# Layer 1 of a two-layer graph attention network: the norm's statistics, W2's last columns and the softmax placed differently

## The chip, the cores and the metric

The kernel runs on one core of one Trainium2 chip. The metric is the device time of one execution in microseconds; the median of 15 runs is given. The core has TensorE (PE; its weight loads are listed as PEld), VectorE (DVE), ScalarE (ACT), GpSimd (POOL) and SyncE (SP), which each work through their own instructions in order and wait for one another by semaphores, and 16 DMA engines.

## The reference

There are 10,000 nodes with 768 features and 170,000 edges (80,000 in both directions and a self loop per node; the network adds a second self loop). One layer of the reference is, cut to what matters:

```python
xl = (x @ W).reshape(n, heads, out_ch)
e = leaky_relu(alpha_src[src] + alpha_dst[dst], 0.2)
e = exp(e - segment_max(e, dst)[dst]);  alpha = e / segment_sum(e, dst)[dst]
out = segment_sum(xl[src] * alpha, dst)

h = gat_conv(x, ..., heads=4, out_ch=256)           # layer 1: 1024 columns
h = relu(layer_norm(h)) + x @ Wr1
h1 = h
h = gat_conv(h, ..., heads=1, out_ch=768)           # layer 2
h = layer_norm(h) + h1 @ Wr2
x = layernorm(x + h)
```

## The kernel before

All arithmetic is in float32. First, x @ W1 is computed for all nodes and stored row by row in a table in DRAM (`table1`: 1024 columns, 4 + 4 attention terms, one number of order), while the nodes are sorted by their number of edges. From then on a *tile* is 128 nodes of like degree, one per partition. There are 79 tiles. A tile has as many *rows* (`SLOTS[t]`) as its largest degree needs; row k of a tile is one gathered table row per node, 128 x 1033 numbers. Tiles are taken in an order in which the sizes first rise (8, 10, 11, ... 26, 41) and then fall (27, ... 11, 9).

Layer 1 (`ordered_layer1`) goes through the tiles in one long unrolled program, whose order on each engine is the order in which it is written (`tc.manual_schedule()`); the tile pools add only the waits. For tile t:

- Rows come through a ring of 29 slots (`Ring`, `RING1`). `ring.fetch` issues a gather on GpSimd's queue (L424) for a row 29 ahead as soon as a row is used up.
- `weights_of(t)` makes the softmax over all rows of a tile: `logits` (L477 to L489: sum, leaky, maximum, difference, exponential on ScalarE, then the rows' numbers are turned into slots for layer 2 and the ring's last columns are set to a large negative number) and `normalised` (L496 to L502). It is started three rows before the end of the tile in front (`LEAD = 3`).
- The first `on_pe(t)` rows are weighted and summed by TensorE: ScalarE makes diagonal matrices (L727), TensorE multiplies them with the rows into `acc` in PSUM (L733).
- The other rows are added to `acc` by VectorE (`weigh`). One row in four VectorE weighs itself, in four instructions (L519); the other three, *shared*, ScalarE scales first (`multiply`, L508) and VectorE adds in one instruction (L515). ScalarE scales at most three rows ahead.
- When tile t's rows are summed, its norm is made at the head of tile t + 1: `deviation` (L577, L579 on VectorE; L581, L582 on ScalarE), `scaled` (L591, L593) and the ReLU with the residual (L804). TensorE transposes the result (`halves`, L705; ScalarE copies it out, L706), multiplies by W2 (L826) and ScalarE copies the two parts (512 and 258 columns) into `row` (`store`, L763), which SP's queue writes to `table2` for layer 2. TensorE also transposes the next tile's x and multiplies it by Wr1 (`product`, L171).

PSUM is full: `acc` has two buffers of two banks, the residual one of two banks, and `half`, which holds transposes and W2's products, two of one bank.

The lines by which the head of a tile is ordered are:

```python
stats = deviation(small, pieces(means[:, :C1], BANK))
...
store(t - 2)
...
xT, moves = from_x(t)
multiplied(first + 2)
...
scaled(h, [means[:, :C1]], stats, g1_b, be1_b)
nc.vector.scalar_tensor_tensor(h, h, 0.0, r_before[:, :C1], op0=OP.max, op1=OP.add)
for move in moves: move()
multiplied(first + LEAD)
```

Layer 2 works in the same manner on `table2` and isn't touched.

Of the kernel before, what the change touches and what calls it, by code (L numbers as in the profile page):

```python
# [35 lines left out]
P = 128  # L36
# [10 lines left out]
RING1 = 29  # L47
RING2 = 41
LEAD = 3
DIAGONALS = 5  # L50
ON_PE2 = 512
SHARE = 4
# [27 lines left out]
def gnn_kernel(ctx, tc, x, x_cols, src, dst, src_col, dst_col, W1, a_src1, a_dst1, b1, g1, be1, Wr1, br1,  # L80
# [390 lines left out]
    def logits(small, ring, lo, hi, ad, heads, c, top=None):  # L471


        n = hi - lo
        e = small.tile([P, ring.size, heads], F32, name="e")[:, :n]
        for a, b, rows in ring.parts(lo, hi):
            nc.vector.tensor_tensor(e[:, a - lo:b - lo], rows[:, :, c + heads:c + 2 * heads],  # L477
                                    ad[:, None, :].to_broadcast([P, b - a, heads]), op=OP.add)
        leaky(e, e)
        new = small.tile([P, heads], F32, name="new")  # L480
        nc.vector.reduce_max(new, e.rearrange("p k h -> p h k"), axis=AX.X)
        if top is not None:
            nc.vector.tensor_max(new, new, top)
        nc.vector.tensor_tensor(e, e, new[:, None, :].to_broadcast([P, n, heads]), op=OP.subtract)  # L484
        nc.scalar.activation(e, e, AF.Exp)  # L485
        for a, b, rows in ring.parts(lo, hi):
            if not ring.own:
                nc.vector.tensor_scalar(slots[:, a:b], rows[:, :, R1 - 1], -1.0, float(NP), op0=OP.mult, op1=OP.min)
                nc.vector.memset(rows[:, :, c + heads:], -BIG)  # L489
        return e, new  # L490

    def normalised(small, e, heads, t):
# [76 lines left out]
    def pieces(a, width):  # L569

        return [a[:, c:c + width] for c in range(0, a.shape[1], width)]

    def deviation(small, parts):

        st = small.tile([P, len(parts), 6], F32, name="st")
        for j, a in enumerate(parts):
            nc.vector.bn_stats(st[:, j, :], a)  # L577
        mv = small.tile([P, 2], F32, name="mv")
        nc.vector.bn_aggr(mv, st.rearrange("p k s -> p (k s)"))  # L579
        sd = small.tile([P, 1], F32, name="sd")  # L580
        nc.scalar.activation(sd, mv[:, 1:2], AF.Ln, bias=eps)  # L581
        nc.scalar.activation(sd, sd, AF.Exp, scale=-0.5)  # L582
        return mv[:, 0:1], sd

    def scaled(to, parts, mean_and_deviation, g, b):

        mean, inv = mean_and_deviation
        c = 0
        for a in parts:
            d = c + a.shape[1]  # L590
            nc.vector.scalar_tensor_tensor(to[:, c:d], a, mean, g[:, c:d], op0=OP.subtract, op1=OP.mult)  # L591
            c = d
        nc.vector.scalar_tensor_tensor(to, to, inv, b, op0=OP.mult, op1=OP.add)  # L593

# [88 lines left out]
    def ordered_layer1():  # L683
        nc.scalar.add_instruction(mybir.InstLoadActFuncSet(name=nc.get_next_instruction_name(), act_func_set_id=6, engine=nc.scalar.engine))
        with tc.tile_pool(name="b1", bufs=1) as pool, tc.tile_pool(name="small1", bufs=2) as small, \
# [32 lines left out]
            def on_pe(t):  # L718


                return min(max(SLOTS[t] // 2 - 5, 1), ON_PE1, SLOTS[t])

            def summed(acc, diagonals, e, q, lo, hi, m):

# [23 lines left out]
                    yield acc  # L748

            def shared(t, k):  # L750
                return (k - on_pe(t)) % SHARE > 0

            last = None
            full = None
            ready = []
            ahead = iter(())

            def store(t):

                nonlocal full  # L760
                row = pool.tile([P, R2], F32, name="row")
                for c, q in full:
                    nc.scalar.copy(row[:, c:c + q.shape[1]], q)  # L763
                full = None
                nc.sync.dma_start(table2[TURNS[t] * P:(TURNS[t] + 1) * P, :], row)


            xT, moves = from_x(0)
            for move in moves:
                move()  # L770
# [1 line left out]
            for t in range(NT + 1):  # L772
# [4 lines left out]
                if whole and not ready:  # L777
                    ahead = weights_of(t)
                    ready += itertools.islice(ahead, 2)

                def multiplied(upto):
                    nonlocal done
                    while whole and done < min(upto, n):
                        if shared(t, done):
                            multiply(ring.slot(FIRST[t] + done), e[:, done], DH1)
                        done += 1

                if whole:
                    e, acc = ready
                if last:  # L790
                    r_before, means = last
                    stats = deviation(small, pieces(means[:, :C1], BANK))
                for _ in ahead:
                    pass
                if full is not None:
                    store(t - 2)
                moves = []
                if live and t:
                    xT, moves = from_x(t)
                multiplied(first + 2)  # L800
                if last:
                    h = pool.tile([P, C1], F32, name="h")
                    scaled(h, [means[:, :C1]], stats, g1_b, be1_b)
                    nc.vector.scalar_tensor_tensor(h, h, 0.0, r_before[:, :C1], op0=OP.max, op1=OP.add)  # L804
                for move in moves:
                    move()
                multiplied(first + LEAD)
                if last:
                    hT = pool.tile([P, K1, P], F32, name="hT")
                    events = [(first + j, move) for j, move in enumerate(halves(hT, h))]  # L810
                def by_wr1():
                    nonlocal r
                    if live and t:
                        r = product(xT, wr1, C1, ps_r)
# [2 lines left out]
                    by_wr1()  # L817

                def to_layer2():
                    nonlocal full  # L820
                    nc.sync.dma_start(h1_d[t - 1], hT.rearrange("p k n -> p (k n)"))
                    full = []
                    for c in range(0, R2, BANK):
                        q = ps_half.tile([P, BANK], F32, name="half")[:, :min(BANK, R2 - c)]
                        for j in range(K1):
                            nc.tensor.matmul(q, hT[:, j, :], w2[:, j, c:c + q.shape[1]],  # L826
                                             start=(j == 0), stop=(j == K1 - 1))
                        full.append((c, q))

                if last:  # L830
                    events.append((first + 2, to_layer2))
# [8 lines left out]
                def due(k):  # L840
                    while events and events[0][0] <= k:
                        events.pop(0)[1]()

                if live and not whole:
                    due(first + 1)
                    sums, acc = (ps_acc.tile([P, 2 * BANK], F32, name="acc") for _ in range(2))
# [11 lines left out]
                                 [by_wr1, lambda: due(n)] + [lambda: None] * n)  # L858
                ready = []
                ahead = iter(())  # L860
                if whole and t + 1 < NT and SLOTS[t + 1] + LEAD <= ring.size:
                    ahead = weights_of(t + 1)
                for k in range(n if whole else 0):
                    multiplied(k + 1 + LEAD)
                    if n - LEAD <= k < n - LEAD + 2:
                        ready += itertools.islice(ahead, 1)
                    if k >= first:
                        weigh(acc, ring.slot(FIRST[t] + k), e[:, k], DH1, shared=shared(t, k))
                    ring.fetch(FIRST[t] + k + 1 + ring.size)
                    due(k)  # L870
                due(DEGREES)
                ready += itertools.islice(ahead, max(2 - len(ready), 0))
                last = None
                if live:
                    last = r, acc
            store(NT - 1)

    def ordered_layer2():
        nonlocal ps_big
# [406 lines left out]
```

## Time and profile before

| | |
|---|---|
| median of 15 runs | 5630.83 us (5619.23 to 5651.92) |
| profiled execution | 5617.48 us, of which the program's span is 5615.6 us |
| mean granted TensorE clock | 0.928 |
| layer 1 within the span | about 906 to 3407 us |
| L515, VectorE adds a scaled row | 801 times, 985.7 us, mean 1231 ns |
| L508, ScalarE scales a quarter of a row | 3284 times, 1341.6 us, mean 523 ns |
| L727 and L733, diagonals and their products | 956 of 389 ns; 1912 passes of 409 ns |
| L577 and L579 in layer 1, statistics | 158 of 689 ns, 79 of 209 ns |
| L424, a gather's issue on GpSimd | 992 ns, 2675 times in both layers |

Durations of one instruction overlap with the next one's on TensorE and ScalarE: a scaling of 523 ns follows the one in front after 405 ns, a TensorE pass over 512 columns after 427 ns. TensorE takes two passes for a float32 product. The waits shown are those of an engine that stood still before an instruction, and name what ended the wait.

### The profile page before, as it was taken

To read this page: it belongs to the slowest core of one execution; us is meant where nothing else is said; L and a number is where in the kernel's file an instruction comes from. 1 tells how busy PE (TensorE), PEld (TensorE's weight loads), DVE (VectorE), ACT (ScalarE), POOL (GpSimd) and SP (SyncE) were. 2 spreads that over 40 slices of the span, in tenths; PEclk is the share of its full clock that TensorE was granted. 3 is DMA by queue.
4 is the path that set the end of the run, shared out by engine and by line. 5 is a ranking of instruction groups with operands and counts; after the bars stand their busy time and mean duration, and the time that the engine had idled before them with its cause. 6 is when DMAs were issued, how large, how long until landed. Compare 5 with 4: busy or idle time off the path is not lost. (4 is left out here: it accounts for less than half of the span.)

```text
span 5615.6 us, 59565 instructions
## 1 busy us (share of the span) xinstructions
PE 4889.6 (87%) x15188; PEld 2892.1 (52%) x15191; DVE 4289.7 (76%) x7729; ACT 2814.5 (50%) x8184; POOL 3235.4 (58%) x3159
## 2 busy tenths in 40 slices
PE   8999996999999875789999999998887747788898
PEld 3444443555555543455555555565555534555555
DVE  5783344999999887888999995887676656767787
ACT  3443444777788776778877762332222222223232
POOL 3447454556666655566665543666666656656663
PEclk9999998999999987899999999998888877889999
DMA  4333536999999986899999986998888878888885
GB/s 156 122 98 87 93 96 255 321 334 355 363 364 372 341 320 249 324 349 359 369 356 352 337 288 251 326 330 313 295 297 286 295 245 302 299 294 309 308 328 198
DMA packets 474306, 1591.37 MB, mean 283 GB/s; under 512 B 118327, under 2 KB 122487, under 8 KB 473958
## 3 DMA queue, kind: packets, MB, share of 16 engines
q0 software_dynamic: 322384, 1286.62, 64.3%
q1 hardware_dynamic: 149520, 297.43, 15.6%
q10 hardware_dynamic: 2054, 3.42, 0.2%
q8 instruction: 128, 2.10, 0.1%
q14 instruction: 220, 1.80, 0.1%
HBM read 1431.80 MB, written 177.29 MB: 287 GB/s over the span
## 5 line engine op out<-in xcount | busy, mean ns | idle before, releaser
L424 POOL DMA_INDIRECT ring<-table,slots x2675 | 2653.8, 992 | 1785.9 <-issue 532.5
L519 DVE SCALAR_TENSOR_TENSOR acc<-ring,e,acc 128x512 f32<-128x512 f32 (+1 forms) x2530 | 1578.4, 624 | 147.1 <-PE acc L733 44.6
L508 ACT ACTIVATE ring<-ring,e 128x256 f32<-128x256 f32 x3284 | 1341.6, 523 | 2.3 <-issue 2.3
L515 DVE TENSOR_TENSOR acc<-acc,ring 128x1024 f32<-128x1024 f32 x801 | 985.7, 1231 | 72.5 <-DVE acc L519 1.8
L952 PE MATMUL big<-wr,w 128*128 128x512 f32 (+1 forms) x2464 | 893.3, 507 | 156.4 <-issue 154.6
L938 PE MATMUL big<-ring,diagonals 128*128 128x256 f32 x2754 | 737.5, 426 | 181.7 <-issue 138.4
L171 PE MATMUL big<-w,xT 128*128 128x512 f32 x1896 | 824.6, 597 | 22.9 <-DMA w<-in_W_dram 9.9
L171 PE MATMUL big<-wr,xT 128*128 128x512 f32 x1896 | 831.2, 595 | 0.2 <-issue 0.2
L826 PE MATMUL half<-w,hT 128*128 128x512 f32 (+1 forms) x2528 | 830.4, 486 | 0.0
L952 PEld LDWEIGHTS big<-wr,w 128*128 128x128 f32 x2464 | 485.2, 198 | 530.9 <-issue 498.9
L938 PEld LDWEIGHTS big<-ring,diagonals 128*128 128x128 f32 x2754 | 583.7, 215 | 337.7 <-issue 204.7
L937 ACT ACTIVATE diagonals<-ident,e 128x128 f32<-128x128 f32 x1377 | 425.0, 391 | 623.8 <-remote 270.4
L826 PEld LDWEIGHTS half<-w,hT 128*128 128x128 f32 x2528 | 477.8, 189 | 372.3 <-issue 334.6
L733 PE MATMUL acc<-ring,diagonals 128*128 128x256 f32 x1912 | 480.4, 409 | 209.4 <-ACT diagonals L727 205.4
L171 PEld LDWEIGHTS big<-w,xT 128*128 128x128 f32 x1896 | 361.7, 191 | 481.4 <-issue 463.3
L171 PEld LDWEIGHTS big<-wr,xT 128*128 128x128 f32 x1896 | 356.1, 191 | 419.0 <-issue 418.9
L733 PEld LDWEIGHTS acc<-ring,diagonals 128*128 128x128 f32 x1912 | 387.4, 205 | 295.4 <-ACT diagonals L727 228.3
L581 ACT ACTIVATE sd<-mv,eps 128x1 f32<-128x1 f32 x237 | 69.5, 293 | 711.5 <-DVE mv L579 423.6
L727 ACT ACTIVATE diagonals<-ident,e 128x128 f32<-128x128 f32 x956 | 293.3, 389 | 205.2 <-DVE e L499 172.0
L665 DVE TENSOR_TENSOR scr<-big,ad_b 128x1024 f32<-128x1024 f32 x79 | 96.7, 1224 | 375.4 <-ACT row L662 319.8
L670 POOL TENSOR_TENSOR row<-row,none 128x1024 f32<-128x1024 f32 x79 | 187.0, 2367 | 261.5 <-ACT row L662 258.2
L485 ACT ACTIVATE e<-e 128x68 f32<-128x68 f32 (+29 forms) x160 | 38.4, 240 | 560.1 <-DVE e L484 228.9
(173 smaller groups left out, 3632.5 us busy)
## 6 DMA issues: line engine op xcount, KB each, us to landing
ring<-table,slots POOLq DMA_INDIRECT x2675
table<-row SPq DMA_DIRECT2D x79, 516.0 KB
h_d<-hT SPq DMA_DIRECT2D x79, 512.0 KB
w<-h_d SPq DMA_DIRECT2D x77, 512.0 KB
table<-row SPq DMA_DIRECT2D x79, 385.0 KB
ring<-table SPq DMA_DIRECT2D x79, 385.0 KB
xT<-in_x_cols_dram SPq DMA_DIRECT2D x79, 384.0 KB
x_d<-xt SPq DMA_DIRECT2D x79, 384.0 KB
```

Source lines behind the costliest of these rows:

```text
L171: nc.tensor.matmul(p[:, c:e], aT[:, j, :], w[:, j, c:e], start=(j == 0), stop=(j == k - 1))
L424: nc.gpsimd.indirect_dma_start(out=to, out_offset=None, in_=table, in_offset=bass.IndirectOffsetOnAxis(ap=index, axis=0), **more)
L508: nc.scalar.activation(row[:, s], row[:, s], AF.Copy, scale=e[:, h:h + 1])
L515: nc.vector.tensor_add(acc[:, :c], acc[:, :c], row[:, :c])
L519: nc.vector.scalar_tensor_tensor(acc[:, s], row[:, s], e[:, h:h + 1], (acc if first is None else first)[:, s], op0=OP.mult, op1=OP.add)
L670: nc.gpsimd.tensor_add(row[:, :C1], row[:, :C1], b1_b)
L727: nc.scalar.activation(diagonals[:, k * H1 + i, :], ident, AF.Copy, scale=e[:, k, i:i + 1])
L733: nc.tensor.matmul(acc[:, c:d], diagonals[:, k * H1 + i, :], ring.slot(q + k)[:, c:d], start=(k == 0 and c % BANK == 0), stop=(k == m - 1 ...
L826: nc.tensor.matmul(q, hT[:, j, :], w2[:, j, c:c + q.shape[1]], start=(j == 0), stop=(j == K1 - 1))
L937: nc.scalar.activation(diagonals[:, k % G, :], ident, AF.Copy, scale=e[:, k, :])
L938: nc.tensor.matmul(to, diagonals[:, k % G, :], ring.slot(FIRST[t] + k)[:, ON_PE2:C2], start=False, stop=(k == n - 1), skip_group_check=True)
L952: nc.tensor.matmul(r[:, c:d], hT[:, j, :], wr2[:, j, c:d], start=False, stop=(j == K1 - 1 and d < C2), skip_group_check=True)
```

## The change

In layer 1:

- The last row of a tile is always a shared one, and its addition on VectorE also gives the sum of `acc` over its 1024 columns (`accum_out=total`). `deviation_about` takes the negated mean from it on ScalarE, squares `acc` less the mean on ScalarE with a sum, and goes on as before. `deviation` remains for the one tile that is too large for the ring.
- The softmax of the next tile is started five rows before the end (`EARLY = 5`) where the ring allows (next tile of up to 22 rows), otherwise four or three. With five, VectorE's first row of the next tile stands before the norm's passes.
- W2's first 512 columns are multiplied where all were; the last 258 follow at the head of the next tile, after x's transposes. The two parts are copied out at two places, and the store follows the second.
- TensorE sums one row less in tiles of 14 to 19 rows (`SLOTS[t] // 2 - 6`).
- The slots and the padding in `logits` are made by GpSimd instead of VectorE.

```diff
-                nc.vector.tensor_scalar(slots[:, a:b], rows[:, :, R1 - 1], -1.0, float(NP), op0=OP.mult, op1=OP.min)
-                nc.vector.memset(rows[:, :, c + heads:], -BIG)
+                nc.gpsimd.tensor_scalar(slots[:, a:b], rows[:, :, R1 - 1], -1.0, float(NP), op0=OP.mult, op1=OP.min)
+                nc.gpsimd.memset(rows[:, :, c + heads:], -BIG)
...
+    def deviation_about(small, total, a, scratch):
+        n = a.shape[1]
+        less = small.tile([P, 1], F32, name="less")
+        nc.scalar.activation(less, total, AF.Copy, scale=-1.0 / n)
+        sd = small.tile([P, 1], F32, name="sd")
+        nc.scalar.activation(scratch, a, AF.Square, bias=less, accum_out=sd)
+        nc.scalar.activation(sd, sd, AF.Ln, bias=eps, scale=1.0 / n)
+        nc.scalar.activation(sd, sd, AF.Exp, scale=-0.5)
+        return less, sd
...
-                return min(max(SLOTS[t] // 2 - 5, 1), ON_PE1, SLOTS[t])
+                return min(max(SLOTS[t] // 2 - 6, 1), ON_PE1, SLOTS[t])
...
-                return (k - on_pe(t)) % SHARE > 0
+                return (k - on_pe(t)) % SHARE > 0 or k == SLOTS[t] - 1
...
+            def first_columns(t, hT):
+                q = ps_half.tile([P, BANK], F32, name="half")
+                for j in range(K1):
+                    nc.tensor.matmul(q, hT[:, j, :], w2[:, j, :BANK], start=(j == 0), stop=(j == K1 - 1))
+                full = t, hT, q
+            def copied():
+                if full:
+                    t, hT, q = full
+                    row = pool.tile([P, R2], F32, name="row")
+                    nc.scalar.copy(row[:, :BANK], q)
+                    full = t, hT, row
+            def last_columns():
+                _, hT, _ = full
+                q = ps_half.tile([P, BANK], F32, name="half")[:, :R2 - BANK]
+                for j in range(K1):
+                    nc.tensor.matmul(q, hT[:, j, :], w2[:, j, BANK:R2], start=(j == 0), stop=(j == K1 - 1))
+                return q
+            def store(q):
+                t, _, row = full
+                nc.scalar.copy(row[:, BANK:], q)
+                nc.sync.dma_start(table2[TURNS[t] * P:(TURNS[t] + 1) * P, :], row)
...
+                    if k == n - 1 and shared(t, k):
+                        nc.vector.scalar_tensor_tensor(acc[:, :C1], row[:, :C1], 1.0, acc[:, :C1], op0=OP.mult,
+                                                       op1=OP.add, accum_out=total)
...
+                begun = first + 1 if whole and early and n - 1 > first else first
+                for k in range(first, begun):
+                    multiplied(k + 1)
+                    weighed(k)
+                    ring.fetch(FIRST[t] + k + 1 + ring.size)
                 moves = []
                 if live and t:
                     xT, moves = from_x(t)
-                multiplied(first + 2)
-                if last:
-                    h = pool.tile([P, C1], F32, name="h")
-                    scaled(h, [means[:, :C1]], stats, g1_b, be1_b)
-                    nc.vector.scalar_tensor_tensor(h, h, 0.0, r_before[:, :C1], op0=OP.max, op1=OP.add)
+                q = last_columns() if full else None
                 for move in moves:
                     move()
+                if last:
+                    scaled(h, [means[:, :C1]], stats, g1_b, be1_b, op)
+                    nc.vector.scalar_tensor_tensor(h, h, 0.0, r_before[:, :C1], op0=OP.max, op1=OP.add)
+                multiplied(first + 2)
+                if q is not None:
+                    store(q)
                 multiplied(first + LEAD)
...
+                    begin = min(max(n - EARLY, n + SLOTS[t + 1] - ring.size + 2), n - LEAD)
+                    early = begin == n - EARLY
```

## The prediction

> **What bounds the kernel now.** I read the page's head first, then the sums by stretch for runs of tiles of equal size (a tile begins at L591, which VectorE executes once per tile), then the timeline around one tile's end, then VectorE's waits. With n I mean a tile's rows per node, with m those of them that TensorE sums.
>
> ```profile
> span 5615.6 us, 59565 instructions
> PE 4889.6 (87%) x15188; PEld 2892.1 (52%) x15191; DVE 4289.7 (76%) x7729; ACT 2814.5 (50%) x8184; POOL 3235.4 (58%) x3159
> ```
>
> The shares are averages. Layer 1 runs from about 906 to 3407 us, and only layer 1 is changed. Stretches of tiles with n = 13 (2 tiles), 17 (4), 20 (3), 22 (2); columns are length, busy PE, PEld, DVE, ACT, POOL, granted clock, DMA share, GB/s:
>
> ```profile
> 1037.00:1089.10 52.10, 50.56 (x168) 29.22 (x167) 48.14 (x80) 39.25 (x103) 29.48 (x29) 1.00 0.91 324
> 1394.00:1512.20 118.20, 112.49 (x383) 67.05 (x381) 109.76 (x179) 91.27 (x245) 74.52 (x72) 1.00 0.97 360
> 1729.90:1830.10 100.20, 91.00 (x307) 55.16 (x306) 90.50 (x145) 81.72 (x220) 64.41 (x64) 0.98 0.97 368
> 1904.30:1984.60 80.30, 63.67 (x205) 39.26 (x204) 66.83 (x107) 57.85 (x155) 46.35 (x46) 0.88 0.90 332
> ```
>
> At n = 17 a tile takes 118.2/4 = 29.55 us, and VectorE works 27.4 of them; the rest is gaps of some 60 ns between its instructions. So VectorE's own chain is the period from n = 14 to 20. At n = 13 and below TensorE is as full. At n = 22 neither is. VectorE's waits in the stretch of n = 22 say why:
>
> ```profile
> DVE e L477 <- DMA ring<-table,slots: 5.8, 2, 3.0
> DVE acc L519 <- PE acc L733: 2.5, 2, 1.6
> ```
>
> The softmax waits for its last gathered row. Now a tile's end and the next one's head at n = 17, engine by engine (start, us):
>
> ```profile
> 1420.46 1.23 DVE L515 TENSOR_TENSOR acc<-acc,ring 128x1024 f32<-128x1024 f32 x1
> 1421.73 1.29 DVE L577 BATCH_NORM_STATS2 st<-acc 128x6 f32<-128x512 f32 x2
> 1423.37 1.28 DVE L591 SCALAR_TENSOR_TENSOR h<-acc,mv,g 128x1024 f32<-128x1024 f32 x1
> 1427.29 2.06 DVE L519 SCALAR_TENSOR_TENSOR acc<-ring,e,acc 128x256 f32<-128x256 f32 x4
> ```
> ```profile
> 1424.91 0.84 ACT L763 COPY row<-half 128x512 f32<-128x512 f32 x2
> 1425.64 1.71 ACT L508 ACTIVATE ring<-ring,e 128x256 f32<-128x256 f32 x4
> 1427.25 0.84 ACT L706 COPY xT<-half 128x512 f32<-128x512 f32 x2
> 1427.98 3.32 ACT L508 ACTIVATE ring<-ring,e 128x256 f32<-128x256 f32 x8
> 1431.18 1.07 ACT L706 COPY hT<-half 128x512 f32<-128x512 f32 x2
> ```
> ```profile
> 1427.87 1.09 PE L705 MATMUL half<-ident,h 128*128 128x128 f32 x8 [1.04 <-ACT xT L706]
> 1428.80 10.46 PE L171 MATMUL big<-wr,xT 128*128 128x512 f32 x24
> 1439.10 10.51 PE L826 MATMUL half<-w,hT 128*128 128x512 f32 x32
> ```
>
> VectorE's first own row (L519, not scaled by ScalarE) stands after the norm's three passes. While it runs, ScalarE gets ahead: the three scaled rows that follow are ready at 1427.35, about 1429.7 and 1431.3, wanted at 1429.45, 1430.75 and 1432.05. The margin is 0.75 to 1 us. The change spends it.
>
> **The change, part by part.**
>
> *VectorE's chain.* Gone are the statistics, 1421.73 to 1423.37, 1.64 us, and the two small instructions for slots and padding (L488, L489), 0.34 us. The last row's addition becomes a scalar-tensor-tensor with a sum: 1.28 (L591's form) for 1.23, and reading the accumulator, 0.083 in its one row (L239): +0.15 with a gap. For n = 14 to 19, m falls by one, so one scaled row more: 3.91/3 = 1.30. Net -0.53 at n = 14 to 19, -1.83 elsewhere, -2.6 where the last row used to be unscaled (2.06 against 1.30: n = 10, 21, 25).
>
> *ScalarE.* Added per tile: the negated mean, like L582, 0.20; a square over 128x1024, between 0.84 (768 wide, L648) and 1.34 (1.02 of L968 scaled from 768 to 1024), I take 1.0 as in L662's copy of this size; the accumulator's read 0.19 (L668). At n = 14 to 19 also four scalings of 0.405 for four diagonals of 0.306. ScalarE has 29.55 - 22.8 = 6.7 us free per tile, so the load is hidden. The order is not. I walk it with T = 0 at the sum of the last row.
>
> ScalarE: mean to 0.25, square and read to 1.5, logarithm and exponential (0.29, 0.20) to 2.1, first xT copy (0.58) to 2.7, second to 2.95, first scaled row (1.65) to 4.6. Next in its order is the copy of W2's last columns. TensorE multiplies those after x's transposes, into the third tile of a pool of two, so it waits until the first xT copy has emptied its half: start 2.75, a weight load 0.2, and 3.68 (10.51 less 16 passes of 0.427), end 6.6. So ScalarE stands still from 4.6 to 6.6; behind that copy (0.38) queue the second and third scaled row, out at 8.75 and 10.35. VectorE: first row 0 to 2.06 (this covers the square, which L603 also waits for), three norm passes 3.92, end 6.0, first scaled row to 7.3, then the second at 8.75 and the third at 10.35 instead of 10.05. **Stall 1.45 + 0.3 = 1.75 us** per tile; 0 if TensorE ran its columns at once after T, 2.3 at the clock of 0.88. After it ScalarE gains about 1 us per four rows, so no further stall.
>
> *TensorE.* m = -1 saves four pairs of 0.454. Splitting W2 takes 3.68 out from before the diagonals. But VectorE's first row, which needs them, now stands before the norm. That closes a loop: h's transposes 6.6 to 7.7 (their second half behind ScalarE's copy), Wr1 10.25, W2's first columns 6.83, diagonals 1.82 m, next T: a period of at least 24.9 + 1.82 m, that is 26.7, 28.5, 30.4, 32.2 for m = 1 to 4. It binds for n up to 13. The wait for sums (L519 <- PE, 0.57 at n = 18 to 20) goes.
>
> *Softmax five rows from the end* (n up to 22; four at 23). The last row of the next tile is gathered after row n + S - 30 of this one (ring of 29, S rows in the next). Before, 26 - S rows of VectorE lie between; after, 24 - S. Waits seen at S = 21 (5 rows): 1.0 and 2.3, later none; at S = 22 (4 rows): 2.8, 3.0, 1.0, 2.1. So S = 20 gets what 22 had, +2.0; S = 21, 3.9 us of rows instead of 7.3, +3.3; S = 22, 3.4 instead of 6.0, +2.4. Bounds: none, and two whole rows of up to 2.06 each, 4.1.
>
> *GpSimd* takes two to four small instructions. Its nearest rows are 0.10 to 0.20 (the MEMSETs at the start) and 2.37 (L670, 128x1024): I take 0.25 each, at most 1 us in a queue with 11 us free per tile. They stand in front of the gather of row n - 5, which waits for VectorE anyway. If that cover went, four gathers behind it would be late by 1 us. The Trainium skill, SBUF — State Buffer, Who interferes with whom, says that a VectorE instruction with two SBUF inputs and a GpSimd one that reads SBUF exclude each other for a whole instruction. The softmax's small additions are such, so by the rule up to 0.25 us per tile, an estimate of 19 us in all, would come on top; my sum leaves it out, and no row of this trace shows it.
>
> The store to the second table goes out some 3 us later on SP's queue; behind it are only the stores of hT and x, read in layer 2.
>
> **Sum** (tiles x change): n = 14 to 17: 29 x (1.75 - 0.53) = 35. n = 18, 19: 14 x (1.75 - 0.53 - 0.57) = 9. n = 20: 6 x (1.75 - 1.83 - 0.57 + 2.0) = 8. n = 21: 4 x (1.75 - 2.6 - 0.9 + 3.3) = 6. n = 22: 4 x (1.75 - 1.83 - 1.25 + 2.4) = 4. n from 23 on, without the early row: about -7. n = 10 to 13 go from 21.6, 24.4, 25.0, 25.9 to 26.7: 5 + 7 + 5 + 4 = 21. Together +76 us on the profiled execution's 5617.5, which lies 13.3 under the median: 5707. That rounds to **5705**, and its own range is 5660 to 5760 (stall 1.0 to 2.3, gathers none to 4.1).
>
> **Rivals.**
> *VectorE's saving stands (faster).* For it: VectorE sets the period, and its chain shrinks by 0.5 to 2.6. Against: the walk. It decides if TensorE starts W2's last columns before T + 0.9, so that ScalarE never waits. With loop and gathers unhindered too: -0.53 x 43, -0.57 x 14, and 2.4, 3.5, 3.1 at n = 20, 21, 22 for 6, 4, 4 tiles, -10 beyond: -82, 5550; with the gather waits as above (35) about 5585. Chance 0.2.
> *The saving eaten by loop and gathers alone.* No stall, but periods floored at 24.9 + 1.82 m and the late rows: 76 less 1.75 x 57 = -24, and the floor gives back 27 at n = 14, 16, 18 and 20 (6 x 1.2, 7 x 0.7, 7 x 1.0, 6 x 1.25): about 5634, no change. Chance 0.1.
> *Gathers become the bound.* DMA stands at 0.97 from n = 16 on; if waits reach n = 17 to 19, 22 tiles x 1.5 = 33 more: 5740. Chance 0.15.
> That the instructions do not move as said is excluded by the changed kernel's order, where W2's 258-column products stand between x's and h's transposes.
>
> **How the numbers follow.** Forecast 0.55, rivals 0.2, 0.1, 0.15. Differences under 0.2%, 11 us, cannot be told from none. Faster: the first rival and a little of the second, 0.22. Same: most of the second, 0.08. Slower: 0.70. The range, 5600 to 5765, leaves out the larger half of the first rival and the far end of the third.
>
> **What would show it.** Right: once per tile VectorE waits some 1.5 us for a scaled row (L516 <- ACT L509), ScalarE's copy L796 waits about 2 us for TensorE, four tiles of n = 17 take near 123 us, the first row of a tile waits for TensorE at n = 13 and below, and the softmax waits for the ring at n = 20 to 22. Wrong: L796 starts without a wait, four such tiles take under 117 us, or layer 1 no longer has VectorE as its fullest engine.

## The result, and the profile after

The changed kernel takes 5811.43 us (median of 8 runs, 5799.93 to 5820.78) against 5630.42 for the kernel before: ratio 1.0319, 95% interval 1.0306 to 1.0331, that is 181 us more. The forecast was 76 more. The page's head after (span, then busy us, share and instructions of each engine):

```profile
span 5810.9 us, 58835 instructions
PE 4899.1 (84%) x14844; PEld 2869.9 (49%) x14847; DVE 4190.8 (72%) x7350; ACT 2953.6 (51%) x8442; POOL 3269.0 (56%) x3407
```

VectorE did lose work, 4289.7 to 4190.8 us, and yet the span grew: its idle time grew by 294 us, three times what it saved. The stretches of the same tiles as before (n = 13, 17, 20, 22; columns as in the prediction):

```profile
1045.10:1097.60 52.50, 48.81 (x158) 27.08 (x157) 44.79 (x71) 40.53 (x106) 29.25 (x35) 1.00 0.89 311
1417.20:1545.30 128.10, 115.12 (x352) 67.08 (x352) 106.94 (x163) 99.92 (x262) 74.57 (x85) 0.93 0.94 332
1773.90:1889.90 116.00, 96.95 (x308) 58.92 (x307) 84.79 (x128) 86.71 (x230) 66.92 (x76) 0.93 0.90 319
1975.90:2057.50 81.60, 59.23 (x177) 34.85 (x176) 61.17 (x91) 58.33 (x154) 43.38 (x51) 0.87 0.84 304
```

Four tiles of n = 17 take 128.1 us, not 118.2 and not the forecast's 123; three of n = 20 take 116.0 instead of 100.2. The granted clock at n = 17, 1.00 before, is 0.93. VectorE's and ScalarE's longest waits (total us, times, longest), in the window from 906 to 3650 us, which is layer 1 and the first 60 us of layer 2:

```profile
DVE acc L516 <- ACT ring L509: 170.1, 131, 4.5
DVE e L478 <- DMA ring<-table,slots: 83.7, 25, 7.6
DVE acc L520 <- PE acc L745: 79.3, 22, 8.7
DVE h L603 <- ACT h L592: 33.5, 8, 10.2
```
```profile
ACT row L796 <- PE half L790: 198.4, 71, 6.5
```

The first line came to 1.2 us in two waits before: rows that ScalarE had scaled were hardly ever late. ScalarE's own wait, for TensorE's last columns of W2, is the forecast's mechanism. At n = 17 it looks like this (VectorE, ScalarE, TensorE; T, the end of the last row, is 1446.86):

```profile
1446.86 2.06 DVE L520 SCALAR_TENSOR_TENSOR acc<-ring,e,acc 128x256 f32<-128x256 f32 x4
1452.68 1.23 DVE L516 TENSOR_TENSOR acc<-acc,ring 128x1024 f32<-128x1024 f32 x1
1457.02 1.23 DVE L516 TENSOR_TENSOR acc<-acc,ring 128x1024 f32<-128x1024 f32 x1 [3.11 <-ACT ring L509]
```
```profile
1447.27 1.11 ACT L592 ACTIVATE h<-acc,less 128x1024 f32<-128x1024 f32 x1
1448.95 0.84 ACT L718 COPY xT<-half 128x512 f32<-128x512 f32 x2
1449.68 1.71 ACT L509 ACTIVATE ring<-ring,e 128x256 f32<-128x256 f32 x4
1455.01 0.38 ACT L796 COPY row<-half 128x258 f32<-128x258 f32 x1 [3.62 <-PE half L790]
```
```profile
1449.57 5.40 PE L790 MATMUL half<-w,hT 128*128 128x258 f32 x16 [3.60 <-ACT xT L718]
```

Up to 1449.57, T + 2.7, the forecast's walk is met to a tenth. Then the sixteen passes take 5.40 us, not 3.68. The windows around them show the granted clock (third number from the end):

```profile
1446.00:1449.50 3.50, 0.00 (x0) 0.00 (x0) 3.39 (x7) 2.37 (x7) 2.54 (x3) 1.00 0.88 319
1449.50:1453.00 3.50, 3.43 (x8) 2.79 (x9) 3.36 (x4) 1.89 (x6) 2.45 (x3) 0.51 0.96 289
1453.00:1456.50 3.50, 3.47 (x19) 2.69 (x19) 0.91 (x1) 1.50 (x5) 1.00 (x1) 1.00 0.99 385
```

After this pause of 3.60 us TensorE runs at half its clock: the passes start 428 to 432 ns apart, then 217 again (this distance is called the pitch below). Of the 79 groups of last columns, 31 follow a pause under 1.5 us, and all of those take 3.75 us or less; of the 48 after a longer pause, 31 take 5.1 to 6.8 us. The shortest pause ahead of such a slow group is 1.86 us. All 18 groups after a pause of 2.74 us or more are slow; of the 30 after one of 1.69 to 2.68 us, 13 are.

At n = 20 the wait is another one (TensorE and VectorE, first three lines below), and at the head of a tile of n = 24 a third (VectorE's last line, and ScalarE):

```profile
1839.28 10.24 PE L745 MATMUL acc<-ring,diagonals 128*128 128x256 f32 x32 [4.85 <-ACT diagonals L739]
```
```profile
1835.41 0.20 DVE L478 TENSOR_TENSOR e<-ring 128x40 f32<-128x40 f32 x1 [3.41 <-DMA ring<-table,slots]
1849.55 2.07 DVE L520 SCALAR_TENSOR_TENSOR acc<-ring,e,acc 128x256 f32<-128x256 f32 x4 [4.86 <-PE acc L745]
2389.82 1.28 DVE L603 SCALAR_TENSOR_TENSOR h<-acc,less,g 128x1024 f32<-128x1024 f32 x1 [4.20 <-ACT h L592]
```
```profile
2383.19 4.78 ACT L739 ACTIVATE diagonals<-ident,e 128x128 f32<-128x128 f32 x16 [2.06 <-DVE e L500]
2388.58 1.11 ACT L592 ACTIVATE h<-acc,less 128x1024 f32<-128x1024 f32 x1
```

At n = 20 the softmax waits for its gathered row, so the diagonals are late, TensorE pauses 4.85 us and sums their 32 products in 10.24 us (8.87 one tile earlier), and VectorE's early first row waits for that. From n = 23 on no row stands ahead of the norm, and its first pass waits for the square, which stands behind all sixteen diagonals.

### The profile page after: what moved, and what is told of

It reads as the page before. It is cut to its first block, busy times and chain, and to the rows that moved or that the text cites. A ratio compares the mean times of both kernels' runs of the same rounds, so it can differ in the third digit from the quotient of the medians.

```text
span 5810.9 us, 58835 instructions
## 1 busy us (share of the span) xinstructions
PE 4899.1 (84%) x14844; PEld 2869.9 (49%) x14847; DVE 4190.8 (72%) x7350; ACT 2953.6 (51%) x8442; POOL 3269.0 (56%) x3407
## 5 line engine op out<-in xcount | busy, mean ns | idle before, releaser
L509 ACT ACTIVATE ring<-ring,e 128x256 f32<-128x256 f32 x3480 | 1425.3, 515 | 0.0
L516 DVE TENSOR_TENSOR acc<-acc,ring 128x1024 f32<-128x1024 f32 x772 | 950.3, 1231 | 219.9 <-ACT ring L509 170.1
L990 ACT ACTIVATE diagonals<-ident,e 128x128 f32<-128x128 f32 x1377 | 425.5, 391 | 646.1 <-remote 266.9
L745 PE MATMUL acc<-ring,diagonals 128*128 128x256 f32 x1568 | 410.1, 422 | 251.3 <-ACT diagonals L739 245.8
L775 PE MATMUL half<-w,hT 128*128 128x512 f32 x1264 | 557.7, 593 | 0.0
L745 PEld LDWEIGHTS acc<-ring,diagonals 128*128 128x128 f32 x1568 | 330.1, 213 | 358.4 <-ACT diagonals L739 282.9
L790 PE MATMUL half<-w,hT 128*128 128x258 f32 x1264 | 354.6, 442 | 156.7 <-ACT xT L718 140.4
L775 PEld LDWEIGHTS half<-w,hT 128*128 128x128 f32 x1264 | 239.7, 190 | 304.2 <-issue 298.9
L790 PEld LDWEIGHTS half<-w,hT 128*128 128x128 f32 x1264 | 273.8, 222 | 225.2 <-ACT xT L718 154.5
L582 ACT ACTIVATE sd<-mv,eps 128x1 f32<-128x1 f32 x159 | 46.5, 292 | 530.2 <-DVE mv L580 257.1
```

The source lines that it names most:

```text
L509: nc.scalar.activation(row[:, s], row[:, s], AF.Copy, scale=e[:, h:h + 1])
L516: nc.vector.tensor_add(acc[:, :c], acc[:, :c], row[:, :c])
L745: nc.tensor.matmul(acc[:, c:d], diagonals[:, k * H1 + i, :], ring.slot(q + k)[:, c:d], start=(k == 0 and c % BANK == 0), stop=(k == m - 1 ...
L775: nc.tensor.matmul(q, hT[:, j, :], w2[:, j, :BANK], start=(j == 0), stop=(j == K1 - 1))
L790: nc.tensor.matmul(q, hT[:, j, :], w2[:, j, BANK:R2], start=(j == 0), stop=(j == K1 - 1))
L990: nc.scalar.activation(diagonals[:, k % G, :], ident, AF.Copy, scale=e[:, k, :])
```

## The experiments

This table sums up the runs. For each it gives the ratio to the kernel before, measured on the same chip, and by how much the periods of layer 1's tiles (from one norm to the next, in the profiled executions) differ from before, summed over tiles of like n: 13, 29, 14, 14 and 8 tiles. The last three rows come from a later session in which the kernel before takes 5333 us (the record gives the chip the same number as for e1, e2, e4 and e5, where it took 5636 us; why it is faster isn't known). By the traces layer 1's tiles take about the same time there, and layer 2 is some 286 us shorter.

| kernel | ratio (95% interval) | n to 13 | 14-17 | 18-19 | 20-22 | from 23 | sum |
|---|---|---|---|---|---|---|---|
| forecast | 1.013 | +21 | +35 | +9 | +18 | -7 | +76 |
| changed kernel | 1.0319 (1.0306-1.0331) | +24 | +58 | +16 | +50 | +36 | +183 |
| e1 columns first | 1.0314 (1.0292-1.0336) | +36 | +15 | +14 | +68 | +34 | +167 |
| e2 columns whole | 1.0559 (1.0538-1.0580) | +74 | +132 | +52 | +34 | +12 | +305 |
| e4 statistics on VectorE | 1.0315 (1.0290-1.0341) | +18 | +69 | +23 | +41 | +32 | +181 |
| e5 filler | 1.0326 (1.0309-1.0343) | +27 | +29 | +38 | +67 | +43 | +204 |
| e3b first row late | 1.0286 (1.0269-1.0303) | +14 | +58 | +11 | +45 | +27 | +155 |
| e3 softmax late too | 1.0326 (1.0306-1.0346) | +11 | +42 | +49 | +45 | +27 | +174 |
| e6 columns first, row late | 1.0230 (1.0208-1.0251) | +12 | +24 | +11 | +59 | +30 | +135 |
| e7 columns whole, row late | 1.0111 (1.0095-1.0128) | +6 | +20 | +6 | +21 | +11 | +65 |
| e8 as e7, statistics on VectorE | 1.0138 (1.0120-1.0157) | +5 | +29 | +8 | +25 | +12 | +78 |
| b1 slots alone | 0.9961 (0.9947-0.9976) | 0 | -11 | -7 | -5 | -1 | -25 |
| b2 split alone | 1.0299 (1.0282-1.0316) | +3 | +40 | +61 | +50 | +25 | +179 |
| b4 early softmax and row alone | 1.0677 (1.0659-1.0695) | +76 | +181 | +88 | +37 | +5 | +388 |
| b5 on_pe alone | 1.0098 (1.0082-1.0113) | +9 | +43 | +7 | +3 | -2 | +60 |
| b6 early softmax alone | 1.0045 (1.0029-1.0060) | +6 | -2 | -1 | +31 | 0 | +34 |
| f1 slots and statistics | 0.9928 (0.9915-0.9942) | +7 | -19 | -9 | -6 | +2 | -25 |

The start of the first tile differs between runs by up to 9 us either way, so sums and ratios differ by as much. In the last three rows layer 1 starts 8 to 9 us earlier, and 8 us of their column "n to 13" are the period of the second tile (n = 10), which gives that back. The profiled execution of e5 is the slowest of its five, 29 us above their median, so its columns may be high by as much.

**First theory**: the order around W2's last columns makes the stall, with half the clock on top.

*e1, columns first.* `store(last_columns())` is moved ahead of `from_x(t)`:

```
-                q = last_columns() if full else None
...
-                if q is not None:
-                    store(q)
+                if full:
+                    store(last_columns())
                 moves = []
                 if live and t:
                     xT, moves = from_x(t)
```

> The changed kernel, with W2's last columns multiplied ahead of x's transposes instead of behind them, and ScalarE's copy of them ahead of its copies of x's transposes. Theory A (ScalarE's copy stands waiting for these columns, and TensorE takes them up after a pause, in part at half its pitch): the copy of 128x258 no longer waits, VectorE's waits for scaled rows (170.1 us in 131 waits) fall under 50, all sixteen passes of the last columns go at the pitch of some 217 ns (3.75 us), and the time falls by 110 to 160 us, to 5650 to 5700. What is then left above the kernel before, 20 to 70 us, belongs to the tiles of n = 20 and more. Rival L (ScalarE simply has too much to do: squares and one scaled row more per tile): the waits for scaled rows keep over 120 us, and the time stays over 5770.

The time stayed (1.0314), and VectorE's waits for scaled rows fell only to 126.6 us, both as rival L had said. Tile by tile it is another matter: at n = 14 to 17 the excess over the kernel before fell from 58 to 15 us and those waits from 95 to 30, and all 79 groups of last columns ran at full pitch. There the theory was right, and the load of ScalarE is not the cause. At n = 20 to 22 the excess rose from 50 to 68 us, below 14 from 24 to 36. From n = 20 on the columns now queue behind the diagonals' products, and ScalarE's copy of them, now ahead of x's copies, waits 137 us instead of 54 (ScalarE's timeline of this run at n = 20, T = 1799.8; the wait ends with x's first transposes, which follow the columns on TensorE):

```profile
1809.44 0.38 ACT L796 COPY row<-half 128x258 f32<-128x258 f32 x1 [7.53 <-PE half L717]
```

*e5, filler.* The transposes of the second half of x are done twelve times for n from 14 on:

```
-                    for i in range(m):
+                    for i in range(m * (again if j else 1)):
```

> The changed kernel with TensorE kept busy: for tiles of n from 14 on, the transposes of the second half of x are done twelve times instead of once (22 more products of 128x128, 2.4 us, in the pause ahead of W2's last columns; the same numbers are written again). Theory H (TensorE runs at half its pitch for about 3.4 us after a pause of some 2 to 4.6 us): the last columns take 3.75 us in nearly all tiles, not 5.4 in about 35 of them, VectorE's waits for scaled rows fall from 170 to about 100, the time falls by 50 to 80 us, to 5730 to 5760, although TensorE does more work. Rival (the slow passes come from something else, such as traffic to the memories at that moment): the last columns keep 5.4 us in some 35 tiles and the time is 5805 to 5850.

At n = 14 to 17 this held: the excess halved, 58 to 29 us, with more work on TensorE. Only two of these 29 groups of columns stayed slow (six of all 79), and VectorE's wait for scaled rows was 1.5 to 2.7 us in 25 of the tiles. In the changed kernel it is 3.2 to 4.8 us in the 23 tiles whose columns ran slow, and 1.8 us in four of the other six (0.4 and 1.4 in two, which had the shortest pauses). The four tiles of n = 17 (window of this run) are back at the full clock:

```profile
1422.20:1543.30 121.10, 116.33 (x439) 70.70 (x437) 107.02 (x164) 99.82 (x262) 74.69 (x85) 1.00 0.97 351
```

The sum of the run was a miss: the time did not fall (5820 us), and over all tiles VectorE's waits for scaled rows rose to 194.8 us. From n = 18 on the filler costs 46 us in this execution; at n = 20, for one, the pause ahead of the columns is 0.46 us in the changed kernel and there is nothing to fill.

*e2, columns whole.* `to_layer2` multiplies all of W2 at once, `store(t - 2)` copies both parts ahead of x's.

> The changed kernel with W2's product in one piece again, as in the kernel before (32 passes, 10.5 us, ahead of the diagonals; both copies ahead of x's). Theory A: VectorE's waits for scaled rows fall under 50 us from 170. But the loop over TensorE's sums, which now runs through VectorE's early first row, gets some 3.1 us longer: a period of at least 28.0 + 1.82 m, that is 29.8, 31.7, 33.5 and 35.3 us for m = 1 to 4. For n = 10 to 13 that is 13 tiles x 3.8 = +50, for 14 and 15 about +8, for 16 to 19 under +20: 5811 - 120 + 75, about 5765 (5720 to 5820). VectorE's waits for TensorE's sums grow from 79 us to over 150. Rival S (the split itself is the harm, by its second copy, its late store and its second weight pass): 5650 or less, and no new waits for sums.

The time rose to 5946 us where 5765 was expected. VectorE's waits for scaled rows fell to 8.7 us, further than expected, but the loop was priced too low: 31.1 us at m = 1 (n = 11, 12) and 33.7 at m = 2 (n = 16), 1.3 to 2 us over the walk (why is open). VectorE's waits in this run:

```profile
DVE acc L520 <- PE acc L745: 363.6, 65, 12.3
```

So without the split the early first row is ruinous, and from n = 20 on, where that loop is not the limit, this run is better than the changed kernel by 40 us.

*e4, statistics on VectorE.*

```
-                return (k - on_pe(t)) % SHARE > 0 or k == SLOTS[t] - 1
+                return (k - on_pe(t)) % SHARE > 0
...
-                if whole and shared(t, n - 1):
-                    total = small.tile([P, 1], F32, name="all")
```

> The changed kernel with the norm's statistics on VectorE again (BATCH_NORM_STATS and its sum, the last row added as in the kernel before). Theory: VectorE gets 1.64 us of work back per tile, but x's copies stand 1.5 us earlier in ScalarE's order and the norm's passes 1.6 us later, so the second scaled row (ready at about T + 6.4, or 8.1 with half the pitch) is wanted at T + 9: VectorE's waits for scaled rows fall from 170 to under 60 us. From n = 23 on, the norm no longer waits for the square behind the diagonals (33.5 us go). Together 5811 + 66 x 1.64 - 115 - 30, about 5775 (5730 to 5800). Rival (the square on ScalarE is itself the cost): under 5700.

No change (1.0315; 5815 us where 5775 was expected), and the waits for scaled rows fell only to 125.9 us. The expectation put x's copies earlier in ScalarE's order; but the deviation's logarithm still stands ahead of them, and now waits for VectorE's statistics (`ACT sd L582 <- DVE mv L580`, 198.4 us in all). That the square is the main cost is out.

**Second theory**: the early first row is a cause of its own at small and large n.

*e3b, first row late*, and *e3, softmax three rows from the end too*:

```
-                    early = begin == n - EARLY
+                    early = False
```
```
-                    begin = min(max(n - EARLY, n + SLOTS[t + 1] - ring.size + 2), n - LEAD)
-                    early = begin == n - EARLY
+                    begin = n - LEAD
```

> The changed kernel with the softmax still five rows from the end, but VectorE's first row behind the norm again, in every tile. Theory B (the early first row waits for TensorE's sums: a loop for n up to 13, and from n = 20 on the chain gather, softmax, diagonals, products, first row): the waits of the first row for TensorE's sums fall from 79 us under 20, n = 9 to 13 lose 20 to 25 us, n of 20 and more some 50; the waits for gathered rows (84 us) stay. At n = 14 to 19 nothing is won, since the norm now waits for the square itself (L603 <- ACT, about 2 us a tile). Together about 5735 (5710 to 5765). Rival O (only the order around W2's last columns costs): 5800 or more, since the norm gets a new wait.

> As the run with the first row late, and the softmax three rows from the end as well, as in the kernel before. If the softmax's place is what makes the gathers late, VectorE's waits for gathered rows fall from 84 us to about 40, as before, and the time falls by a further 20 to 35 us, to about 5710 (5685 to 5740). Rival (the wait only moves from the softmax to the products of the diagonals): the same time as the run with the first row late, within 10 us, and the waits for TensorE's sums up by as much as the gathers' fall.

Both missed, with 5789 and 5807 us. The waits for sums went, but others took their place. VectorE's in the first of the two:

```profile
DVE h L603 <- ACT h L592: 134.3, 69, 9.0
DVE e L478 <- DMA ring<-table,slots: 114.6, 28, 25.8
DVE acc L516 <- ACT ring L509: 98.6, 93, 4.6
```

The 25.8 us at the end of the second line are one wait for the very first rows, which every kernel has and which lies in this window by chance. Without it the gathers' wait is 88.8 us. At n = 20 to 22 the scaled rows, which had kept VectorE waiting for 15 us, now did so for 43. With the softmax late too, the gathers' wait fell to 46 us (72.7 with the first rows' 26.5), as expected, and the norm's wait for the square rose to 184.5, since all the diagonals now stand ahead of it. VectorE in that run, at a tile of n = 18, and what ScalarE did in the meantime:

```profile
1572.92 1.28 DVE L603 SCALAR_TENSOR_TENSOR h<-acc,less,g 128x1024 f32<-128x1024 f32 x1 [3.03 <-ACT h L592]
```
```profile
1567.46 3.61 ACT L739 ACTIVATE diagonals<-ident,e 128x128 f32<-128x128 f32 x12 [2.84 <-DVE e L500]
1570.98 0.56 ACT L783 COPY row<-half 128x512 f32<-128x512 f32 x1
1571.68 1.11 ACT L592 ACTIVATE h<-acc,less 128x1024 f32<-128x1024 f32 x1
```

The wait had only moved.

*e6, columns first and first row late* (both edits).

> W2's last columns ahead of x's transposes and VectorE's first row behind the norm, in one kernel. If the two causes are separate (order around the columns at n = 14 to 17, early first row at n up to 13 and from 18 on), the gains add: 43 us at n = 14 to 17, 25 below, 30 to 50 above, less about 1 us a tile for the square that the norm now waits for at n = 14 to 19: 5710 to 5740. If they are one (whichever is taken away, the other wait takes its place), the time stays within 20 us of the run with the first row late alone.

5764: the gains added in part. n = 14 to 17 stayed low (24 us), n from 20 on high (89): ScalarE's copy waits 125 us there, much as in e1.

**Third theory**: split and early row hide each other, one wait standing ready behind the other.

*e7* is e2 with `early = False`; *e8* is e7 with the edit of e4.

> Two parts undone at once: W2's product in one piece, and VectorE's first row behind the norm. Each of them alone left the time near 5800 or over it. Theory M (each hides the other: the split makes ScalarE's scaled rows late, and without the split the early first row waits for TensorE): both waits go at once, VectorE's waits for scaled rows (98.6 us with the first row late alone) fall under 30, those for TensorE's sums (363.6 us with the unsplit product alone) under 40. What stays is the norm's wait for the square (some 130 us in L603), one scaled row more at n = 14 to 19, and the gathers: 5695 (5670 to 5725). Rival: the square on ScalarE, which stands ahead of x's copies in all versions so far, is what makes the scaled rows late: the waits for them stay over 70 us and the time over 5740.

> As the run before it in this list (product whole, first row late), with the norm's statistics on VectorE too. Left of the change are the softmax five rows from the end, one row less on TensorE at n = 14 to 19, and the small instructions on GpSimd. Theory: 43 tiles x (1.30 - 0.34) = 41 us more at n = 14 to 19, some 15 us for later gathers at n = 20 to 22, so 5685 (5660 to 5710), near the run with the square on ScalarE, since 1.64 us of VectorE's work takes the place of a wait of some 2 us. Rival (the square is the main cost): under 5640.

They took 5683 and 5694 us, within 12 and 9 of what was expected. VectorE's waits in the first:

```profile
DVE e L478 <- DMA ring<-table,slots: 129.7, 30, 26.6
DVE h L603 <- ACT h L592: 85.2, 53, 3.7
DVE h L603 <- issue: 42.2, 25, 3.7
DVE acc L516 <- ACT ring L509: 24.5, 51, 0.9
```

The longest is again for gathered rows, 26.6 us of it for the very first ones; the norm's two lines together are 127 us, where some 130 were expected. Together the two parts hold some 120 of the 181 us, and undoing the early row alone gave 19, the split alone minus 135.

**Each part alone on the kernel before.** *b2* has only the split (`first_columns`, `copied`, `last_columns`, `store(q)` as in the diff); *b4* only `EARLY`, with the first row ahead of the norm; *b1* only the two small instructions moved to `nc.gpsimd`.

> The kernel before, with W2's product split as in the change (last columns one tile later, between x's and h's transposes, their copy on ScalarE behind the first scaled row), and nothing else. Walked like the forecast, T = 0 at the end of the last row: statistics and deviation to 2.2, second half of the diagonals to 3.4, x's copies to 4.6, first scaled row to 6.2, last columns from about 4 to 7.7 (9.4 at half the pitch), copy, second scaled row out at 9.8 to 11.5, wanted at 8.9: a stall of 0.9 to 2.6 us a tile from n = 14 on, 65 tiles, so 60 to 170 us more: about 5730 (5690 to 5800). Rival (ScalarE has room for it as long as the square isn't there): under 5650.

> The kernel before, with the softmax five rows from the end and VectorE's first row ahead of the norm, and nothing else. By the loop over TensorE's sums with W2 in one piece (periods of 31.8 us at m = 1 and 33.7 at m = 2 in the run with the product unsplit) and one row more on TensorE than there at n = 14 to 19 (m = 2 to 4: 33.7, 35.5, 37.3): n = 10 to 13: +70, 14 and 15: +90, 16 and 17: +100, 18 and 19: +85, above: +40. Together some 385 us more, about 6010 (5930 to 6060). Rival (VectorE starts its next tile earlier and keeps busy while the norm waits): under 5700.

> The kernel before, with the two small instructions for slots and padding on GpSimd and nothing else changed. By the forecast's sum: 0.34 us off VectorE's chain in the 43 tiles of n = 14 to 19 that are bound by it, and nothing elsewhere: 15 us less, 5615 (ratio 0.997). Rival (GpSimd and VectorE keep each other out of memory, or the gathers behind them are late): no gain, ratio 1.000 to 1.005.

b2: 1.0299, 5788 us where about 5730 was expected. The split costs as much alone as the whole change, without square, early row or half clock (78 of 79 groups at full pitch). ScalarE and TensorE at n = 17, T = 1437.35:

```profile
1439.40 1.27 ACT L727 ACTIVATE diagonals<-ident,e 128x128 f32<-128x128 f32 x4
1442.31 0.86 ACT L706 COPY xT<-half 128x512 f32<-128x512 f32 x2 [1.65 <-PE half L705]
1446.73 0.38 ACT L783 COPY row<-half 128x258 f32<-128x258 f32 x1 [1.97 <-PE half L777]
```
```profile
1439.84 2.00 PE L733 MATMUL acc<-ring,diagonals 128*128 128x256 f32 x8 [1.45 <-ACT diagonals L727]
1442.95 3.75 PE L777 MATMUL half<-w,hT 128*128 128x258 f32 x16 [0.46 <-ACT xT L706]
```

The second half of the diagonals, which exists for m = 3 and 4 only, pushes x's transposes and the columns back; n = 14 and 15 (m = 2) lose next to nothing (2.4 us in 14 tiles), n = 16 and 17 2.5 us a tile. b4 came within 4 us of its 6010: 6007, by the loop (VectorE's waits for TensorE's sums are 384 us). b1 gained 22 us (ratio 0.9961) and beats both kernels.

What stayed open then was what e7's remaining 62 us are, and the statistics' own worth:

> The kernel before with one row less on TensorE (n//2 - 6 for n//2 - 5) and nothing else. By the forecast's term: one more scaled row on VectorE at n = 14 to 19, 29 x 1.30 = 38, and 14 x (1.30 - 0.57) = 10 at n = 18 and 19, where the wait for TensorE's sums goes: 48 us more, 5680 (5660 to 5700). Rival (TensorE and ScalarE, relieved of diagonals, give it back): 5640 or less.

> The kernel before with the softmax five rows from the end, VectorE's first row staying behind the norm, and nothing else. By the forecast's term: the last gathered row is late by 1.0 us at n = 19, 2.0 at 20, 3.3 at 21, 2.4 at 22 (7, 6, 4 and 4 tiles): 42 us; the waits for TensorE's sums (22 us at n = 18 to 22) go in return, as the diagonals are earlier: 20 to 42 us more, about 5660 (5645 to 5680). Rival (the wait is only moved from the sums to the gathers): within 10 us of the kernel before.

> The kernel before with two parts of the change that do not touch the order of TensorE's work: the small instructions on GpSimd (22 us gained alone) and the norm's statistics on ScalarE, with the last row always shared. Statistics took 11 us less in the pair of runs with and without them (product whole, first row late). If the two add: 5595 (5580 to 5610), ratio 0.994, the fastest of all. Rival (without the earlier diagonals the square stands behind more of ScalarE's work and the norm waits over 2.5 us a tile): 5620 to 5660.

*b5* changes `// 2 - 5` to `// 2 - 6`: 50 us at n = 14 to 19 (43 + 7) where the forecast's term gave 48. *b6* is b4 with `early = False`: 1.0045, 23 us in that session, with 31 in the tiles of n = 20 to 22. *f1* puts `deviation_about` with the last row's `accum_out`, and b1's edit, into the kernel before: 0.9928, faster than before, its interval below b1's.

e7 holds the parts of b5, b6 and f1. Alone they add up to 0.7%, together they cost 1.1%: some 20 of e7's 62 us come from their working together, and are open.

## Why the prediction was wrong

The sign was right, and at n up to 19 the mechanism; the size was not: 183 us in the tiles for 76. The table splits VectorE's time between one norm and the next, changed kernel less kernel before, in the profiled executions (us; in brackets the forecast's term where it had one; gaps of up to 0.15 us are counted as own work). The columns in the middle are VectorE's waits by what it was about to take up.

| n | own work | scaled rows | first own row, for TensorE's sums | gathered rows | norm | other | sum |
|---|---|---|---|---|---|---|---|
| to 13 | -31 | +10 | +24 | 0 | +11 | +10 | +24 (+21) |
| 14-17 | -39 (-15) | +95 (+51) | 0 | 0 | 0 | +2 | +58 (+35) |
| 18-19 | -18 (-7) | +34 (+25) | -3 (-8) | +4 | 0 | -1 | +16 (+9) |
| 20-22 | -41 (-29) | +14 (+25) | +39 (-12) | +35 (+35) | +2 | 0 | +50 (+18) |
| from 23 | -16 | +23 | -8 | +9 | +27 | +1 | +36 (-7) |

By the forecast's own steps:

1. **n up to 13, the loop** (25 + 1.82 m): 24 us for 21. Right; b4's 6007 for 6010 rests on the same loop, with the periods measured in e2.
2. **n = 14 to 17, "the second scaled row at 8.75", stall 1.75.** The walk was right up to the start of the last columns, and the stall in most tiles where they ran at full pitch (1.8). On average it was 3.3 us (95 in 29 tiles). The term that failed is the columns' price, "3.68 (10.51 less 16 passes of 0.427), end 6.6": taken from columns that ran without a pause ahead of them, while the same walk left TensorE idle until T + 2.75. In 23 of these 29 tiles they ran at half the clock, and the filler (e5) removed that part: 58 us to 29. For its upper stall of 2.3 us the forecast used a clock of 0.88, the mean of a whole stretch; right behind the pause 0.51 was granted. That the sum missed by only 23 us is in part luck, since VectorE's own work shrank by 39 us, not 15. The Trainium skill, TensorE: Matmul & The Clock Gate, section HAM oscillation, warns of TensorE's idle gaps of more than some 3.4 us; a rule against this change that the prediction should have weighed. All 17 groups after 3.6 us or more agree with it; here 1.86 us were enough in part of the cases, so the measurement is the stricter.
3. **n = 20 to 22, +18 foreseen, +50 measured; from 23 on, -7 foreseen, +36 measured.** This is the larger error, 75 of the 107 us. The walk of n = 17 was carried over to tiles where more stands between T and the columns. At n = 20 to 22 the late gathers cost VectorE the 35 us that were priced. The term that failed is the wait for TensorE's sums, which was to go (-12) and grew by 39: the forecast priced the late gather as a wait of VectorE alone, and not the chain behind it, that is diagonals, TensorE's pause, products, and the first row that had been put in front of the norm. From 23 on it took the stall of tiles without an early row as nothing; the scaled rows cost 23 us there, and b2 shows that the split alone makes them late without any early row (25 us). And the square behind sixteen diagonals (4.2 us), most of the 27 us at the norm, was not looked at.
4. **VectorE's saving as a sum of -1.83 a tile.** The parts came out as follows: slots -22 us (b1; 0.34 us by 43 to 77 tiles is 15 to 26), one row less on TensorE +50 (b5) for 43 x 1.30 less 14 x 0.57, that is 48; the softmax's place +23 (b6) for 35 of late gathers less 12 of sums that no longer wait, 23. In sum these terms were right, the last one by luck: in b6's trace both its parts are larger, gathers +63 and sums -28. The statistics, priced at 1.64 us, gave 11 to 19 us in all (e7 against e8, f1 against b1; the latter pair by ratios, from two sessions): without a row to cover it, the norm waits for the square instead of for the statistics (117.6 us in f1). The early row that was to cover it cost more than it covered.
5. **The rule on ports** (the Trainium skill, SBUF — State Buffer, Who interferes with whom), kept out of the sum with an estimate of 19 us: b1 gives no sign of it, its gain being the full 22.
6. **The rival "VectorE's saving stands"** needed columns that start before T + 0.9; e1 moved them ahead of that (at n = 17 they start at 1447.35 for a T of 1449.06) and took three quarters of the excess at n = 14 to 17, but the place that is right at n = 17 is wrong at n = 20.

Open are why 17 of the 30 groups after pauses of 1.69 to 2.68 us ran at full pitch and 13 did not (in e4 one did even after 3.48 us), why e2's loop is 1.3 to 2 us longer than the walk, and why VectorE's own work shrank by more than was priced.

## What to carry to other kernels

Take a duration only from a row that has the same idle time ahead of it as the place to which the work is moved. Walk the order for every size of tile at which the number of pieces changes (here m from 2 to 3, and the tiles without an early row), not for one of them. And where undoing one part leaves the time as it was, undo pairs: two waits of like length stand in for each other, and only the pair (e7) and the parts alone (b1 to b6) showed what each was worth.

## What the runs showed that was not expected

TensorE at half its clock after 13 of 30 pauses of 1.69 to 2.68 us and after all 18 longer ones in the changed kernel, 0.51 granted over the 3.5 us right behind such a pause, with 0.93 as the mean of a stretch that had 1.00. The 22 extra transposes of a filler, idle work of 2.4 us, were repaid at n = 14 to 17 by 1 us a tile. And two small instructions of VectorE, 0.34 us a tile, were worth 0.4% of the kernel when moved alone, while the change that contained them lost 3%.
